# Attention and a mixture of experts on one core: where the moments, one copy and two output products stand in the queues

## The chip, the cores and the metric

The kernel runs on one core of one Trainium2 chip. A core has five engines, each with its own queue that is worked off in order: TensorE (PE, matrix products; PEld is its weight load), VectorE (DVE), ScalarE (ACT), GpSimd (POOL) and SyncE (SP), which here only issues transfers. ScalarE and GpSimd issue transfers too. The metric is the device time of one execution in microseconds (us); lower is better. All numbers are float32.

## The reference

The input has 8 sequences of 1024 rows, 256 wide. All rows are normalised, and the output is the input plus two branches of the normalised rows: a causal linear attention with 16 heads, and a mixture of 8 experts of which each row uses 2.

```python
xn = _layernorm(x, axis=-1)

# attention: q, k, v are products of xn with 256 x 256 weights, 16 heads of 16
q = jax.nn.elu(q) + 1.0
k = jax.nn.elu(k) + 1.0
kv_cumsum = jnp.cumsum(jnp.einsum('blhd,blhe->blhde', k, v), axis=1)
out = jnp.einsum('blhd,blhde->blhe', q, kv_cumsum)
denom = jnp.clip(jnp.einsum('blhd,blhd->blh', q, jnp.cumsum(k, axis=1)), 1e-06, None)
attention = (out / denom[..., None]).reshape(Bx, Lx, HIDDEN) @ Wo.T

# experts: the two best of 8 by xn @ Wr, weighted by the softmax of the two
gate = jnp.einsum('bsh,ehi->besi', xn, W1)          # W1, W3: 8 x 256 x 512
up = jnp.einsum('bsh,ehi->besi', xn, W3)
y = jnp.einsum('besi,eih->besh', jax.nn.silu(gate) * up, W2)   # W2: 8 x 512 x 256
experts = jnp.einsum('bse,besh->bsh', c, y)

return x + attention + experts
```

## The kernel before

**Blocks and tiles.** The 8192 rows are 16 blocks of 512 rows (`NBLK`), each of 4 pieces of 128 rows (`NCH`). The experts' work is in tiles of 128 rows that share one expert: `NM` = 132 tiles, of which the first `N1` = 25 are listed from the first four blocks alone (`first_batch`) and the others from all rows (`second_batch`, made while tiles 12 to 21 run).

**Of each block.** `moments(t, n)` computes mean and reciprocal deviation of n blocks on VectorE: per piece a statistics instruction (L283) and its aggregate (L284), then once per call some 17 small dependent instructions for the reciprocal square root. It reads `xb`, the loaded rows. `normalise` (L318, ScalarE for these blocks) applies them, `turn` (L333) transposes the block on TensorE and stores it, and `load_x(t + 5)` on ScalarE's queue loads a later block into the buffer that came free. `logits` (L356), `add_logits` and, every fourth block, `route` choose the experts. In the loop over tiles, tile j first normalises and turns block t = 4 + j (up to block 15).

**Attention of a block** is a generator, `block_steps`, with 9 steps. Steps 0 to 3 project q, k, v (L795, L811), turn k (L858), and make the denominators (L880 on TensorE, L886 and L887 on VectorE), which go through DRAM in five transfers on SP. Step 4 computes the first piece's `scores` (L917): products into four PSUM buffers, all that the pool `ps_mm` has, which VectorE then masks one by one into `s_sb` (L924). Steps 5 to 8 take the pieces c = 0 to 3 in turn: the scores of piece c + 1, then `weigh` of piece c (L943, L951, L961 on TensorE; `oT` L968, and the new state, L971 and L980, on VectorE). `attend` is the output product of one piece: four matmuls with `wo_sb` (L993), a copy by ScalarE into the tile `at` (L998, one buffer), and, after piece 3, one transfer by GpSimd that adds the block into DRAM (L1003): into `acc_d` for the first four blocks as long as `acc_d` has not been copied to the output, else into the output. The `attend` of piece 3 is left in the list `behind` and done in the next block's step 0, after its two q projections. `attend_upto` says how many steps are made by tile j; from tile 22 on it is some 1.14 a tile.

**Of each tile** (`ffn_step`): gathers of its rows by GpSimd four tiles ahead (L1178, L1183), its weights W1 and W3 two tiles ahead on SP (L1244, five buffers), the hidden products `gu_ps` (L1263, two PSUM buffers of `ps_mm`), SiLU on ScalarE (L1271) and the product on VectorE (L1274, `hT`), the output product `y_ps` of the tile before (L1282), its scaling on VectorE (L1289) and an adding scatter by GpSimd (L1293). From tile 27 on the rows are turned by a transfer on SP (`ffn_turn_halves`, L1209; issued with the weights of the same tile, two tiles ahead) instead of on TensorE (L1228), with a copy by VectorE ahead of it (L1200) and one by ScalarE behind it (L1218, `xgT`).

**One copy.** The first 25 tiles and the attention of the first blocks are added up in `acc_d`. At tile `N1 + 1` = 26, `acc_d` is copied to the first 2048 rows of the output by a transfer on SP (L1382), 2 MB read and 2 MB written. It has to wait for all that was added into `acc_d` before it, and what is added to the output comes after it.

**What sets the order.** Outside the first part, which is in written order, a planner puts the instructions of each engine in order at compile time: it runs the program by its own estimate of times and lets each engine take, of what is ready by that estimate, what stands first in the text. On the chip each queue then keeps that order, and an instruction that waits holds all behind it. `in_order` pins an instruction behind what stands before it on its engine; all of SP's transfers are pinned so. `tc.issue_after(ins)` puts what its block writes on `ins`'s engine behind `ins` in the queue, without waiting for its end. Before, the moments in the loop are put behind `last_token`, the last instruction of the first batch's list.

Of the kernel before, what the change touches and what calls it, by code (L numbers as in the profile page):

```python
# [51 lines left out]
ALU = mybir.AluOpType  # L52
# [12 lines left out]
def tile_attention_moe(  # L65
# [14 lines left out]
    nc = tc.nc  # L80
    B, L, H = x.shape
    E, _, I = w1.shape
# [751 lines left out]
    def project(t):  # L834


        if t > 0:
            begin(t)
            for o in range(KC):
                for _ in project_q(t, o):  # L840
                    pass
                mask_q(t, o)
                yield
            for c in range(0, NCH, 2):
                for _ in project_k(t, c):
                    pass
                yield
        else:
            for _ in range(4):
                yield  # L850
        qT, qm, kT, kn, va, rden = blocks[t]
        upto_t = two.tile([P, KC], F32, tag="upto_t", name="upto_t")
        fresh = t % BLK_PER_SEQ == 0
        qks = []
        for o in range(KC):
            tp = ps_t.tile([P, TB], F32, tag="t", name="tp")
            for c in range(NCH):
                nc.tensor.transpose(  # L858
                    tp[:, bass.ts(c, P)], kn[:, c, bass.ts(o, P)], ident
                )  # L860
            nc.scalar.copy(kT[:, o, :], tp)
            ksum = two.tile([P, TB], F32, tag="ksum", name="ksum")
            nc.vector.tensor_tensor_scan(
                ksum, ones[:, 0:1].to_broadcast([P, TB]), kT[:, o, :],
                0.0 if fresh else sums[0][:, o : o + 1], ALU.mult, ALU.add,
            )
            nc.vector.tensor_copy(upto_t[:, o : o + 1], ksum[:, TB - 1 : TB])
            nc.vector.tensor_tensor(ksum, qT[:, o, :], ksum, ALU.mult)
            qks.append(ksum)
            yield  # L870
        for c in range(0, NCH, 2):
            if t > 0:
                for _ in project_v(t, c):
                    pass
            yield

        den = ps_y.tile([P, P], F32, tag="y", name="den")
        for o in range(KC):
            for c in range(NCH):
                nc.tensor.matmul(  # L880
                    den[32 * c : 32 * c + 32, :], lhsT=own_of[:, o, :],
                    rhs=qks[o][:, bass.ts(c, P)], start=(o == 0), stop=(o == KC - 1),
                    skip_group_check=True,
                )
        over = one.tile([P, P], F32, tag="over", name="over")
        nc.vector.tensor_scalar(over, den, EPS_DEN, None, ALU.max)  # L886
        nc.vector.reciprocal(over, over)  # L887

        through = den_d[t % 2]
        for c in range(NCH):  # L890
            in_order(
                nc.sync.dma_start(
                    out=through[HEADS * c : HEADS * (c + 1)],
                    in_=over[32 * c : 32 * c + HEADS, :].unsqueeze(1).to_broadcast([HEADS, HD, P]),
                )
            )
        in_order(
            nc.sync.dma_start(
                out=rden.rearrange("p c o l -> p (c o) l"),
                in_=through.rearrange("(x h) d l -> (h d) x l", h=HALF),  # L900
            )
        )
        yield
        del xnTs[t]
        sums[0] = upto_t

    state = [None]

    def scores(t, c):

        qT, qm, kT, kn, va, rden = blocks[t]
        span = bass.ts(c, P)
        s_ps = [ps_mm.tile([P, KC, 2, P], F32, tag="mm", name="s_ps") for r in range(4)]
        for hh in range(KC):
            for r in range(4):
                rows = slice(32 * r, 32 * r + 32)
                nc.tensor.matmul(  # L917
                    s_ps[r][:, hh].rearrange("p a l -> p (a l)"), lhsT=kT[rows, hh, span],
                    rhs=qm[rows, hh, :, span], start=True, stop=True,
                )  # L920
        s_sb = []
        for r in range(4):
            sm = masked.tile([P, KC * 2, P], F32, tag="s_sb", name="s_sb")
            nc.vector.tensor_tensor(  # L924
                sm, s_ps[r].rearrange("p k a l -> p (k a) l"), causal_b, ALU.mult
            )
            s_sb.append(sm)
        return t, c, s_sb

    def weigh(t, c, s_sb):  # L930

        qT, qm, kT, kn, va, rden = blocks[t]
        first = t % BLK_PER_SEQ == 0 and c == 0
        last = t % BLK_PER_SEQ == BLK_PER_SEQ - 1 and c == NCH - 1
        span = bass.ts(c, P)
        both_ps = ps_t.tile([P, KC * P + KC * PAIR], F32, tag="t", name="o_ps")
        o_ps = both_ps[:, 0 : KC * P].rearrange("p (k l) -> p k l", k=KC)
        kv_ps = both_ps[:, KC * P :].rearrange("p (k d) -> p k d", k=KC)
        before_c = state[0]
        if not first:  # L940
            for hh in range(KC):
                for r in range(4):
                    nc.tensor.matmul(  # L943
                        o_ps[32 * r : 32 * r + 32, hh, :],
                        lhsT=before_c[:, hh, 32 * r : 32 * r + 32], rhs=qT[:, hh, span],
                        start=(hh == 0), stop=False, skip_group_check=True,
                    )
        for hh in range(KC):
            for a in range(2):
                for r in range(4):  # L950
                    nc.tensor.matmul(  # L951
                        o_ps[32 * r : 32 * r + 32, hh, :],
                        lhsT=va[:, c, 4 * hh + r, a, :],
                        rhs=s_sb[r][:, 2 * hh + a, :],
                        start=(first and a == 0), stop=(a == 1), skip_group_check=True,
                    )

        if not last:
            for hh in range(KC):
                for r in range(4):  # L960
                    nc.tensor.matmul(  # L961
                        kv_ps[32 * r : 32 * r + 32, hh, :],
                        lhsT=kn[:, c, hh * P + 32 * r : hh * P + 32 * r + 32],
                        rhs=own_v(va, c, 4 * hh + r, 4 * hh + r + 1),
                        start=True, stop=True, skip_group_check=True,
                    )
        oT = two.tile([P, KC, P], F32, tag="oT", name="oT")
        nc.vector.tensor_tensor(oT, rden[:, c], o_ps, ALU.mult)  # L968
        if not last:
            new = three.tile([P, KC, P], F32, tag="kv", name="kv")  # L970
            nc.vector.tensor_tensor(  # L971
                new.rearrange("p k (g d) -> p k g d", d=PAIR),
                kv_ps.unsqueeze(2).to_broadcast([P, KC, 4, PAIR]),
                heads.rearrange("p (g d) -> p g d", d=PAIR).unsqueeze(1).to_broadcast(
                    [P, KC, 4, PAIR]
                ),
                ALU.mult,
            )
            if not first:
                nc.vector.tensor_tensor(new, new, before_c, ALU.add)  # L980
            state[0] = new
        return oT
# [26 lines left out]
    def block_steps(t):  # L1009


        for i, _ in enumerate(project(t)):
            if i == 1 and behind:
                attend(*behind.pop())
            if i in (1, 3, 5, 8):
                yield
        if t + 1 < NBLK:
            fetch(t + 1)
        waiting = scores(t, 0)
        yield  # L1020
        done = None
        for c in range(NCH):
            coming = scores(t, c + 1) if c + 1 < NCH else None
            if done and c + 1 < NCH:
                attend(*done)
            oT = weigh(*waiting)
            if done and c + 1 == NCH:
# [308 lines left out]
    for j in range(NM + 1):  # L1336
# [7 lines left out]
            for _ in routing:  # L1344
                pass
        if 0 < j and t < NBLK:
            if j % 2 == 0:
                with tc.issue_after(last_token[0].ins):
                    for _ in moments(t, 2):
                        pass  # L1350
            normalise(t)
            turn(t)
            if t + 5 < NBLK:
# [20 lines left out]
        if j < LISTS:  # L1374
            attend_upto(3 + j // 2)
        elif j < READ:
            attend_upto(AHEAD - 3 * (READ - j - 1) // 2)
        else:
            attend_upto(AHEAD + (NBLK * STEPS - AHEAD) * (j - READ + 1) // (NM - READ - 4))
        if j == N1 + 1:  # L1380
            copied.append(j)
            in_order(nc.sync.dma_start(out=out_rows[0 : FT * P, :], in_=acc_d[:, :]))  # L1382
        ffn_step(j, LATE if N1 < j <= N1 + LATE else 0)
    assert steps_made[0] == NBLK * STEPS
    while stored[0] < NM:
        ffn_store(stored[0])
# [51 lines left out]
```

## Time and profile before

| what | value |
|---|---|
| time, median of 7 runs | 1284.06 us (1278.55 to 1287.39) |
| the profiled execution's own time | 1285.06 us |
| its span, first to last instruction | 1283.3 us |
| mean granted TensorE clock | 0.989 |
| TensorE busy, weight load busy | 1219.4 us, 1049.6 us |
| VectorE, ScalarE, GpSimd busy | 674.3, 553.8, 523.4 us |
| HBM read and written | 196.30 MB, 52.67 MB |

A line such as "L1263" is line 1263 of the kernel. A timeline's row gives the start (us from the span's start), the duration, the engine, line and operation, what is written from what, how many instructions were merged, and in brackets how long the engine was idle before and what ended the wait ("issue": nothing that the profile shows). In the lists of waits the columns are the total in us, how often, and the longest. The chain of waits is followed back from the last instruction, at each step to what released it; its rows give start, duration and what. Matmuls overlap at their ends, so distances are read from start to start. The granted clock is the share of TensorE's full clock that was given; 0.5 is half speed.

### The profile page before, as it was taken

How to read it: one execution, taken by the hardware profiler on the slowest of the kernel's cores; microseconds unless marked ns; L12 is line 12 of the kernel's file. 1: busy time of each engine (PE TensorE's matmuls, PEld its weight loads, DVE VectorE, ACT ScalarE, POOL GpSimd, SP SyncE). 2: the span in 40 equal slices, each digit the busy share in tenths (PEclk: the TensorE clock that was granted, in tenths of full speed). 3: DMA queues.
4: the chain of work that ended last, by engine and by line, in shares of the span. 5: the costliest groups of instructions: out<-in, count | busy, mean ns of one | idle time of the engine just before them, and what ended most of it. 6: DMA issues, size and time to landing. Idle time of an engine off the chain costs nothing.

```text
span 1283.3 us, 30887 instructions
## 1 busy us (share of the span) xinstructions
PE 1219.4 (95%) x12102; PEld 1049.6 (82%) x12102; DVE 674.3 (53%) x1541; ACT 553.8 (43%) x1060; POOL 523.4 (41%) x460
## 2 busy tenths in 40 slices
PE   5689999999999999999999999999999999999995
PEld 4568887778888888888888888888888888888885
DVE  7766579863344454535453544445454536354541
ACT  5565465371532526262625344252626262444420
POOL 3633334323444444344343435444434435343432
PEclk9899999999999999999999999999999999999998
DMA  9797565557798798889696979988788979787984
GB/s 339 256 290 226 174 191 154 188 135 241 181 234 199 179 210 188 208 187 220 161 222 158 225 164 216 191 173 229 175 208 193 213 166 216 171 219 161 204 194 68
DMA packets 220593, 254.30 MB, mean 198 GB/s; under 512 B 73218, under 2 KB 144514, under 8 KB 220162
## 3 DMA queue, kind: packets, MB, share of 16 engines
q1 hardware_dynamic: 177058, 198.08, 53.2%
q0 software_dynamic: 38064, 43.22, 24.1%
q10 hardware_dynamic: 5328, 11.01, 2.4%
q8 instruction: 99, 1.62, 0.5%
q14 instruction: 44, 0.36, 0.1%
HBM read 196.30 MB, written 52.67 MB: 194 GB/s over the span
## 4 chain that ended last, share of the span: by engine, by line
PE 86%; DVE 6%; DMA 4%; ACT 2%; SPq 1%; issue 1%; POOL 0%; POOLq 0%; ACTq 0%; DVEq 0%
PE gu_ps L1263 37%; PE y_ps L1282 17%; PE a_ps L993 5%; PE s_ps L917 5%; PE o_ps L951 4%; PE zkv L811 4%; PE zkk L811 4%; PE zq L795 4%; PE o_ps L943 2%; DMA xb<-in_x_dram 1%; DMA acc_d<-in_x_dram 1%; PE tp L858 1%; DVE s_sb L924 1%; DVE at_place L573 1%; SPq L1138 1%
## 5 line engine op out<-in xcount | busy, mean ns | idle before, releaser
L1263 PE MATMUL gu_ps<-xgT,w 128*128 128x128 f32 x4224 | 513.7, 279 | 18.9 <-DVE s_sb L924 12.0
L1263 PEld LDWEIGHTS gu_ps<-xgT,w 128*128 128x128 f32 x4224 | 494.1, 194 | 35.6 <-DVE s_sb L924 16.4
L1293 POOL DMA_INDIRECT out_dram<-y,dst_i x107 | 177.2, 1656 | 282.1 <-issue 56.8
L1282 PE MATMUL y_ps<-w_sb,hT 128*128 x1056 | 250.8, 380 | 1.4 <-DVE hT L1274 1.4
L1178 POOL DMA_INDIRECT xg<-in_x_dram,src_i x132 | 128.7, 975 | 288.9 <-DVE half L1200 160.1
L1271 ACT ACTIVATE hT<-gu_ps 128x512 f32<-128x512 f32 x132 | 78.8, 597 | 318.7 <-PE gu_ps L1263 318.3
L1282 PEld LDWEIGHTS y_ps<-w_sb,hT 128*128 128x128 f32 x1056 | 190.3, 190 | 23.2 <-DVE hT L1274 1.0
L924 DVE TENSOR_TENSOR s_sb<-s_ps,causal 128x512 f32<-128x512 f32 x256 | 162.6, 682 | 71.6 <-PE o_ps L951 40.0
L1274 DVE TENSOR_TENSOR hT<-gu_ps,hT 128x512 f32<-128x512 f32 x132 | 90.4, 685 | 69.6 <-PE gu_ps L1263 44.1
L1183 POOL DMA_INDIRECT entry<-tab_d,of_i x107 | 106.4, 994 | 38.7 <-issue 32.2
L1289 DVE TENSOR_SCALAR y<-y_ps,entry 128x256 f32<-128x256 f32 x132 | 63.6, 482 | 111.3 <-PE y_ps L1282 111.0
L1200 DVE COPY half<-xg 128x512 uint16<-128x512 uint16 x105 | 45.7, 435 | 139.9 <-ACT xg L1190 139.8
L998 ACT COPY at<-a_ps 128x256 f32<-128x256 f32 x64 | 23.6, 369 | 156.6 <-PE a_ps L993 156.6
L917 PE MATMUL s_ps<-qm,kT 32*128 32x256 f32 x1024 | 85.8, 403 | 0.5 <-DVE hT L1274 0.4
L1218 ACT COPY xgT<-halfT 128x512 uint16<-128x512 uint16 x105 | 79.6, 758 | 3.2 <-DMA halfT<-half 3.2
L1190 ACT ACTIVATE xg<-xg,entry 128x256 f32<-128x256 f32 x132 | 78.6, 596 | 4.7 <-DMA xg<-in_x_dram,src_i 4.7
L993 PE MATMUL a_ps<-wo_sb,oT 128*128 128x256 f32 x256 | 70.0, 396 | 2.1 <-DVE oT L968 2.1
L917 PEld LDWEIGHTS s_ps<-qm,kT 32*128 32x128 f32 x1024 | 51.2, 184 | 24.5 <-issue 19.6
L951 PE MATMUL o_ps<-s_sb,va 128*32 128x128 f32 x2048 | 68.9, 273 | 0.0
L1293 POOL DMA_INDIRECT acc_d<-y,src_i x25 | 42.8, 1712 | 59.2 <-DVE y L1289 25.7
L993 PEld LDWEIGHTS a_ps<-wo_sb,oT 128*128 128x128 f32 x256 | 44.7, 189 | 24.1 <-issue 14.5
L811 PE MATMUL zkk<-wkv_sb,xnT 128*128 128x256 f32 x256 | 59.5, 381 | 0.0
(213 smaller groups left out, 1331.3 us busy)
## 6 DMA issues: line engine op xcount, KB each, us to landing
w<-in_w_dram SPq DMA_DIRECT2D x264, 512.0 KB
den_d<-over SPq DMA_DIRECT2D x64, 128.0 KB
rden<-den_d SPq DMA_DIRECT2D x16, 512.0 KB
xnT_d<-xnT ACTq DMA_DIRECT2D x15, 512.0 KB
xnT<-xnT_d SPq DMA_DIRECT2D x15, 512.0 KB
out_dram<-in_x_dram SPq DMA_DIRECT2D x12, 512.0 KB
out_dram<-at POOLq DMA_DIRECT2D x12, 512.0 KB, 9.6
xb<-in_x_dram SPq DMA_DIRECT2D x10, 512.0 KB
```

The lines of the kernel that those rows point to most:

```text
L811: nc.tensor.matmul(z[:, i, :], lhsT=xnTs[t][:, k, bass.ts(c + i, P)], rhs=wkv_sb[:, k, a, :], start=(k == 0), stop=(k == KC - 1),)
L917: nc.tensor.matmul(s_ps[r][:, hh].rearrange("p a l -> p (a l)"), lhsT=kT[rows, hh, span], rhs=qm[rows, hh, :, span], start=True, stop=True,)
L924: nc.vector.tensor_tensor(sm, s_ps[r].rearrange("p k a l -> p (k a) l"), causal_b, ALU.mult)
L951: nc.tensor.matmul(o_ps[32 * r : 32 * r + 32, hh, :], lhsT=va[:, c, 4 * hh + r, a, :], rhs=s_sb[r][:, 2 * hh + a, :], start=(first and a = ...
L993: nc.tensor.matmul(a_ps, lhsT=oT[:, hh, :], rhs=wo_sb[:, hh, :], start=(hh == 0), stop=(hh == 1),)
L1178: nc.gpsimd.indirect_dma_start(out=xg[j], out_offset=None, in_=x_rows[:, :], in_offset=bass.IndirectOffsetOnAxis(ap=src_i[:, i : i + 1], a ...
L1183: nc.gpsimd.indirect_dma_start(out=entry[j], out_offset=None, in_=table[:, :], in_offset=bass.IndirectOffsetOnAxis(ap=num_i[:, i : i + 1], ...
L1218: nc.scalar.copy(xgT[j].bitcast(U16).rearrange("p k (l b) -> p b k l", b=2), halves.pop(j).rearrange("p (b k) l -> p b k l", b=2),)
L1263: done = nc.tensor.matmul(ps[:, i, :], lhsT=w13[:, k, bass.ts(i, P)], rhs=xgT[j][:, k, :], start=(k == 0), stop=(k == KC - 1),)
L1274: nc.vector.tensor_tensor(hT, gu[1], hT, ALU.mult)
L1282: done = nc.tensor.matmul(y_ps, lhsT=hT[:, i, :], rhs=w2_sb[:, bass.ds(e * (IC * H) + i * H, H)], start=(i == 0), stop=(i == IC - 1),)
L1293: nc.gpsimd.indirect_dma_start(out=rows[:, :], out_offset=bass.IndirectOffsetOnAxis(ap=dst_i[:, i : i + 1], axis=0), in_=ys.pop(j), in_off ...
```

## The change

Four things are moved; the arithmetic stays.

- The moments in the loop: instead of a call for blocks t and t + 1 ahead of `normalise(t)` in tiles 2, 4, 6, 8 and 10, there are calls after the attention steps of tiles 0 (block 6), 2, 4, 6, 8 (blocks 7 and 8, 9 and 10, 11 and 12, 13 and 14) and 10 (block 15). They are put behind `last_masked`, the attention's VectorE instruction written last (`over`, `s_sb` or `oT`); in tile 0 behind `last_token` as before.
- The copy from `acc_d` to the output is written behind `ffn_step(26)`, whose transfers on SP are tile 28's weights and its transpose.
- The output product of a block's piece 3 is written behind the next block's first scores (step 4) instead of in its step 0.
- The output product of piece 1 is written ahead of the scores of piece 3 instead of behind them.

```diff
         nc.vector.tensor_scalar(over, den, EPS_DEN, None, ALU.max)
-        nc.vector.reciprocal(over, over)
+        last_masked[0] = nc.vector.reciprocal(over, over)
...
     state = [None]
+    last_masked = [None]
...
             sm = masked.tile([P, KC * 2, P], F32, tag="s_sb", name="s_sb")
-            nc.vector.tensor_tensor(
+            last_masked[0] = nc.vector.tensor_tensor(
...
-        nc.vector.tensor_tensor(oT, rden[:, c], o_ps, ALU.mult)
+        last_masked[0] = nc.vector.tensor_tensor(oT, rden[:, c], o_ps, ALU.mult)
...
         for i, _ in enumerate(project(t)):
-            if i == 1 and behind:
-                attend(*behind.pop())
             if i in (1, 3, 5, 8):
                 yield
         if t + 1 < NBLK:
             fetch(t + 1)
         waiting = scores(t, 0)
+        if behind:
+            attend(*behind.pop())
         yield
         done = None
         for c in range(NCH):
+            if c == 2:
+                attend(*done)
             coming = scores(t, c + 1) if c + 1 < NCH else None
-            if done and c + 1 < NCH:
+            if c == 1:
                 attend(*done)
             oT = weigh(*waiting)
...
         if 0 < j and t < NBLK:
-            if j % 2 == 0:
-                with tc.issue_after(last_token[0].ins):
-                    for _ in moments(t, 2):
-                        pass
             normalise(t)
             turn(t)
...
+        if j % 2 == 0 and j + 1 < LISTS:
+            ahead = (t + 2, 1) if j == 0 else (t + 1, min(2, NBLK - t - 1))
+            with tc.issue_after((last_masked if j else last_token)[0].ins):
+                for _ in moments(*ahead):
+                    pass
+        ffn_step(j, LATE if N1 < j <= N1 + LATE else 0)
         if j == N1 + 1:
             copied.append(j)
             in_order(nc.sync.dma_start(out=out_rows[0 : FT * P, :], in_=acc_d[:, :]))
-        ffn_step(j, LATE if N1 < j <= N1 + LATE else 0)
```

## The prediction

> **What bounds the kernel now.** I read the page first, then TensorE's waits, then the chain of waits and the timelines around each wait.
>
> ```profile
> PE 1219.4 (95%) x12102; PEld 1049.6 (82%) x12102; DVE 674.3 (53%) x1541; ACT 553.8 (43%) x1060; POOL 523.4 (41%) x460
> ...
> PE 86%; DVE 6%; DMA 4%; ACT 2%; SPq 1%; issue 1%; POOL 0%; POOLq 0%; ACTq 0%; DVEq 0%
> ```
>
> TensorE works 95% of the span and carries 86% of the chain. The change removes no matmul, so all it can win is TensorE's idle time (64 us, some 25 of them in the first 60 us and 12 behind the last matmul, which nothing here touches), time at a reduced clock, and small losses where one kind of matmul follows another. The waits of TensorE, 320 to 1230 us (waited for: us in total, times, longest):
>
> ```profile
> PE gu_ps L1263 <- DVE s_sb L924: 5.3, 8, 0.7
> PE gu_ps L1263 <- issue: 4.0, 5, 0.8
> PE gu_ps L1263 <- ACT xgT L1218: 2.0, 1, 2.0
> ```
>
> The first two are one place, once in each of blocks 3 to 15: 13 waits, 9.3 us. After a block's first scores there is nothing behind them on TensorE but the next tile's `gu_ps`, whose PSUM buffer is held until VectorE has masked `s_ps`. On TensorE's timeline (start, us, engine, line):
>
> ```profile
> 652.23 1.15 PE L917 MATMUL s_ps<-qm,kT 32*128 32x256 f32 x16
> 654.18 3.81 PE L1263 MATMUL gu_ps<-xgT,w 128*128 128x128 f32 x32 [0.81 <-issue]
> ...
> 692.05 1.03 PE L993 MATMUL a_ps<-wo_sb,oT 128*128 128x256 f32 x4
> 692.92 1.28 PE L1263 MATMUL gu_ps<-xgT,w 128*128 128x128 f32 x10
> ```
>
> The last two rows are the output product of the block's last piece, at a place where TensorE waits for nothing: it takes 692.92 - 692.05 = 0.87 us there.
>
> The third wait comes from SP's queue. Its waits and its timeline:
>
> ```profile
> SPq L1382 <- DMA acc_d<-at: 9.8, 1, 9.8
> ```
>
> ```profile
> 337.63 0.39 SPq L1244 DMA_DIRECT2D w<-in_w_dram  x1
> 347.96 0.55 SPq L1382 DMA_DIRECT2D out_dram<-acc_d  x1
> 349.12 1.07 SPq L1244 DMA_DIRECT2D w<-in_w_dram  x1
> 350.24 1.32 SPq L1209 DMA_TRANSPOSE halfT<-half  x1
> ```
>
> The rows' copy stands 9.8 us at the head of SP's queue until block 2's attention has been added into `acc_d`. Tile 28's weights and transpose are behind it. The chain then runs 8.70 us through that transpose, ends in the 2.0 us wait, and tile 28's 32 `gu_ps` matmuls take 5.46 us instead of 3.8.
>
> The longest wait behind the start is at 88.46 us, 5.90 us, after the first scores of block 0. VectorE's timeline and the chain there:
>
> ```profile
> 86.11 0.29 DVE L406 TENSOR_TENSOR same<-lg_all,best 128x128 f32<-128x128 f32 x1
> 90.27 0.43 DVE L283 BATCH_NORM_STATS2 st<-xb 128x6 f32<-128x256 f32 x1 [3.87 <-DMA xb<-in_x_dram]
> ...
> 93.63 0.68 DVE L924 TENSOR_TENSOR s_sb<-s_ps,causal 128x512 f32<-128x512 f32 x1
> ```
>
> ```profile
> 94.36 5.06 PE gu_ps L1263 x22
> ...
> 107.37 2.65 PE gu_ps L1263 x22
> ```
>
> The moments of block 12 wait in VectorE's queue for a load of x that was issued at 80.80. The masks are behind them, so `gu_ps` starts at 94.36. Then 22 matmuls take 5.06 us where 22 take 2.65 later: the granted clock is 0.65 from 94.4 to 103.0, which is 0.35 x 8.6 = 3.0 us lost. Likewise it is 0.73 from 360 to 366, 0.27 x 6 = 1.6 us, after the 2.0 us wait.
>
> **1. Moments behind attention's VectorE work.** Block 12's moments move from the planner's early place to behind piece 0's `oT` (tile 6; at 118 before), long after their load. Without them the queue from 86.40 holds eight routing and eviction steps that cost 1.8 us interleaved (chain pieces 0.28 + 0.40 + 0.19 + 0.19 + 0.19 + 0.18 + 0.24 + 0.13) and some 2.5 us alone, as dependent steps add 0.03 to 0.1 us each. The first mask then runs from 88.9 to 89.5 and `gu_ps` starts at 89.6: 94.36 - 89.6 = 4.8 us. The wait left is 1.1 us, and waits up to 1.37 us (at 240.3) show no lower clock, so the 3.0 us go too: 7.8 us. The ceiling is 5.9 + 3.4 (the clock loss from 93.6 on) = 9.3.
>
> What it costs: moments now come one tile ahead of their use. A pair of blocks takes VectorE 8 x 0.48 (statistics and their aggregate) + 17 x 0.20 (the square root's chain) = 7.2 us; `normalise` adds 4 x 0.5 on ScalarE. Queued behind them on VectorE are the tile's `hT` and `y`; waiting for them are `normalise`, the transposes of `turn`, and through `turn` the ACT-issued load of x five blocks on, which still has some 10 us. Six calls instead of five add 17 x 0.20 = 3.4 us, covered by VectorE's idle time from 130 to 160 us. Of these, one end shows: before, `turn(15)` ran at 163.99, 3.25 us behind piece 2's last VectorE step (160.74); now 4 x 0.48 + 3.4 + 2.0 = 7.3 us lie between, so routing and the second batch's lists start 4.1 us later against TensorE. From 180 to 260 VectorE is 91% busy and TensorE waits for it in small pieces. Bounds: 0 (TensorE has other work) to 4.1 us; I take 2.0, the middle, as both are nearly full there. Net gain 5.8 us.
>
> **2. The copy behind a tile's weights.** `w(28,0)` and its transpose can then go at 339.4, when tile 25's last weights come free, and `w(28,1)` at 344.4. The output product of block 2's last piece also moves from tile 26 to tile 29, after the copy; so it is added to `out_dram` and the copy waits only for tile 24's store (issued 336.22, landing median 6.3 us). `xgT(28)` is then limited by ScalarE, whose SiLU of tile 27 ends at 355.8; with 0.76 us it is there at 356.6, before the preceding transposes end at 357.75. Gain 2.0 + 1.6 = 3.6 us; bound 0 if the transpose is still late. The copy's 4 MB move some 3 us earlier, the scatter into `out_dram` with them.
>
> The Trainium skill, "TensorE: Matmul & The Clock Gate", Part 1, has the clock fall only after an idle window of about 3.4 us. The row above disagrees: 2.0 us sufficed. By the page this term would be 2.0 instead of 3.6 and the forecast 1.6 us higher.
>
> **3. The last piece's output product behind the next block's first scores.** At step 0 the 0.87 us go. At step 4 `s_ps` to `gu_ps` takes 654.18 - 652.23 = 1.95 us now. With the product between: 1.08 (677.00 to 678.08 below) + 0.97 (`a_ps` to `gu_ps` behind narrow matmuls, 406.44 to 407.41) = 2.05, while the mask is ready at 1.95. Net 0.87 - 0.10 = 0.77 us, 13 times: 10.0 us. Blocks 1 and 2 have no such gap (`y_ps` lies there): 0. Bounds 0 to 13 x 0.87 = 11.3.
>
> Each moved product brings its ScalarE copy and POOL's add along. `at` has one buffer. Now its copy ends near 725.3, POOL's store and gather put the add's issue near 726.8, it lands 9.6 us later (row of part 6), at 736.4; the next block's first copy into `at` comes at 740.1. Even if the add waited for the store issued at 723.85 to land (5.7 us), it would land at 739.2. ScalarE's next work behind that copy is a SiLU at 743.7. So 0 us; it costs once it is 4 us later still. POOL's store behind the add waits for it as now (7.7 us), with rows gathered four tiles ahead.
>
> **4. Piece 1's product ahead of piece 3's scores.** Now:
>
> ```profile
> 677.00 1.15 PE L917 MATMUL s_ps<-qm,kT 32*128 32x256 f32 x16
> 678.08 1.13 PE L993 MATMUL a_ps<-wo_sb,oT 128*128 128x256 f32 x4
> 679.14 0.64 PE L943 MATMUL o_ps<-qT,kv 128*32 128x128 f32 x16
> ```
>
> `a_ps` costs 1.06 us between two narrow kinds (679.14 - 678.08); behind `y_ps` it is wide after wide, 0.87. 0.2 us, 13 times: 2.6 us; bounds 0 to 2.6.
>
> **Sum.** 5.8 + 3.6 + 10.0 + 2.6 = 22.0 us. The profiled execution took 1285.06 us (span 1283.3), 1.0 above the median of 1284.06. 1284.06 - 22.0 = 1262.
>
> **Rivals.** (a) Slower: the wait moves from the masks to the transposes. If the planner keeps `turn` ahead of the next tile's `gu_ps`, TensorE meets it 5.9 us after the tile before starts (3.84 + 0.38 + 1.73), but piece work ends 1.3 us in, and moments and `normalise` need 9.2 more: 4.6 us each for four pairs and 2.7 for the single block 15, 21 us, with 1.6 us of clock each 29. Less 7.8 + 3.6 + 12.6 that is 5 us slower, 1289; it decides from 4 us a call. For it: all ten blocks' moments now sit one tile from use. Against it: the planner already splits `tp` and puts `lg_ps` inside `gu_ps` by readiness. (b) The product lands ahead of the scores, as the planner takes what is ready; then its 0.87 us only moves and 13 gaps stay: 1272. Against: in pieces 1 and 2 the order written is scores, product, and so it ran. (c) The early gain is given back wholly by the late lists and transposes: 1268. (d) The copy's order alone does nothing, the transpose limits it: 1266.
>
> **How the numbers follow.** Likeliest case 0.62: 1262, own range 1256 (ceilings 9.3 + 3.6 + 11.3 + 2.6 = 26.8, less a little spread) to 1270 (4.1 us of lists, no gain from 4, part of 2 missing). (b) 0.10; (c), (d) and mixtures of them 0.10; several failing at once, within 0.3% of no change, 0.05; (a) and its like 0.13. Range 1256 to 1278, which takes in (b), (c) and (d) mixed. Faster 0.82, same 0.05, slower 0.13; 0.3%, 3.9 us, is about what a measurement of this kernel can tell.
>
> **What would show it.** Right: no `st` waits for x ahead of an `s_sb`; clock full at 94 to 103 and 360 to 366; no L1382 wait ahead of `w(28)`; `s_ps`, `a_ps`, `gu_ps` without a gap once a block, and blocks 69.3 instead of 70.3 us apart. Wrong: TensorE waits at `tp` L333 for `xb` L318, `a_ps` ahead of the first `s_ps`, ScalarE's `at` waiting for the add, or wider gaps from 180 to 300 us.

## The result, and the profile after

The changed kernel takes 1297.57 us (median of 19 runs, 1288.85 to 1305.37) against 1283.46 us (46 runs of the kernel before beside it, 1278.55 to 1289.18): a ratio of 1.0102, 95% interval 1.0087 to 1.0117. By the ratio that is 13 us slower, where 22 us faster was forecast. The profiled execution took 1296.67 us, with a span of 1295.0 us and a mean clock of 0.979 (1285.06, 1283.3 and 0.989 before). Line numbers shift: `gu_ps` is L1266, `y_ps` L1285, `a_ps` L994, `s_ps` L918, `s_sb` L925, `oT` L969, the copy L1387.

Engines and the chain of waits, from the page after:

```profile
PE 1226.5 (95%) x12102; PEld 1053.0 (81%) x12102; DVE 680.1 (53%) x1558; ACT 557.3 (43%) x1062; POOL 522.3 (40%) x460
...
PE 80%; DMA 9%; DVE 7%; ACT 2%; issue 1%; SPq 1%; POOL 0%; POOLq 0%; DVEq 0%; ACTq 0%
```

TensorE still works 95% of the span, but the chain has moved: TensorE carries 80% instead of 86%, transfers 9% instead of 4%. So a transfer that was hidden is no longer hidden. TensorE's waits from 320 to 1230 us (total, times, longest) name it:

```profile
PE a_ps L994 <- DVE oT L969: 6.8, 6, 2.0
PE gu_ps L1266 <- DVE s_sb L925: 0.4, 1, 0.4
```

Of the 13 waits of 9.3 us behind the scores one of 0.4 us is left, about as forecast, and the wait for `xgT` is gone. In their place stand six waits for `oT`. Both on TensorE's timeline:

```profile
534.36 1.15 PE L918 MATMUL s_ps<-qm,kT 32*128 32x256 f32 x16
537.54 1.39 PE L994 MATMUL a_ps<-wo_sb,oT 128*128 128x256 f32 x4 [2.04 <-DVE oT L969]
...
661.91 1.15 PE L918 MATMUL s_ps<-qm,kT 32*128 32x256 f32 x16
662.99 1.13 PE L994 MATMUL a_ps<-wo_sb,oT 128*128 128x256 f32 x4
663.96 3.73 PE L1266 MATMUL gu_ps<-xgT,w 128*128 128x128 f32 x32
```

The last three rows are what the change wanted, in block 7: scores, product and next tile without a gap, 2.05 us from `s_ps` to `gu_ps`, just the 1.08 + 0.97 of the prediction. The first two are the new loss, in block 5. The timelines of VectorE, GpSimd and SP there:

```profile
519.02 0.95 DVE L887 RECIPROCAL over<-over 128x128 f32<-128x128 f32 x1
...
537.07 0.42 DVE L969 TENSOR_TENSOR oT<-rden,o_ps 128x256 f32<-128x256 f32 x1 [3.35 <-DMA rden<-den_d]
```

```profile
522.46 1.41 POOL L1004 DMA_DIRECT2D out_dram<-at  x1 [1.41 <-DMA out_dram<-y,dst_i]
```

```profile
527.60 0.37 SPq L898 DMA_DIRECT2D rden<-den_d  x1
```

`oT` needs the denominators back from DRAM. They come 18.0 us after their reciprocal here, where it took 13.2 to 14.9 us in blocks 3 to 14 of the kernel before and 15.3 in block 15. In between, at 522.46 us, GpSimd issues the 512 KB add of the previous block, which the moved product brought along. In this block the four writes end in the usual time (the read is issued 8.6 us behind the reciprocal, 7.3 to 8.9 before) and the read is late, 9.4 us from issue to landing instead of 5.7 to 7.3. In blocks 3, 6 and 14 it is the writes that are late: the read is issued 10.5 to 11.4 us behind the reciprocal.

At the start, the masks are no longer held, but TensorE waits elsewhere (first TensorE's longest wait from 60 to 130 us, then VectorE's timeline, last the row of before for block 7):

```profile
PE tp L333 <- ACT xb L318: 4.6, 2, 4.3
```

```profile
77.11 0.69 DVE L283 BATCH_NORM_STATS2 st<-xb 128x6 f32<-128x256 f32 x2
...
83.70 0.68 DVE L925 TENSOR_TENSOR s_sb<-s_ps,causal 128x512 f32<-128x512 f32 x1
...
86.73 0.15 DVE L305 SCALAR_TENSOR_TENSOR tab<-mv,tab 128x8 f32<-128x8 f32 x1
```

```profile
48.34 0.39 DVE L283 BATCH_NORM_STATS2 st<-xb 128x6 f32<-128x256 f32 x1
```

The moments of blocks 7 and 8 begin at 77.11 us, behind the denominators' reciprocal; before, block 7's ran from 48.34. They end at 86.9, ScalarE normalises only then, and TensorE waits 4.3 us for the transposes of block 7. The clock is at half for 13.7 us (84.3 to 98.0) instead of 6.8 (93.6 to 100.4), and tile 4 starts at 98.1 us instead of 94.36.

The second batch's lists begin later as well. Their first VectorE step, before and after:

```profile
175.42 0.16 DVE L517 TENSOR_SCALAR rows_i<-count 128x8 int32<-128x8 f32 x1
```

```profile
186.75 0.16 DVE L517 TENSOR_SCALAR rows_i<-count 128x8 int32<-128x8 f32 x1
```

The copy, on SP's timeline, no longer waits at the head of the queue:

```profile
355.63 0.39 SPq L1247 DMA_DIRECT2D w<-in_w_dram  x1
356.13 0.55 SPq L1387 DMA_DIRECT2D out_dram<-acc_d  x1
```

The start of tiles, after less before, shows where it all lies: +3.7 us at tile 4, some +12 from tile 16 to 23, +7.3 at tile 29 (the copy's gain, and the clock is full from 360 to 366), then slow gains eaten by the `oT` waits, +4.3 at the last tile. The last matmul ends at 1275.34 instead of 1271.04, but the end comes 19.6 us behind it instead of 12.2; this stretch is called the tail below. On GpSimd's timeline:

```profile
1222.37 1.40 POOL L1004 DMA_DIRECT2D out_dram<-at  x1 [4.54 <-DMA out_dram<-y,dst_i]
...
1282.99 1.54 POOL L1296 DMA_INDIRECT out_dram<-y,dst_i  x1 [2.95 <-DMA out_dram<-y,dst_i]
1287.54 1.55 POOL L1296 DMA_INDIRECT out_dram<-y,dst_i  x1 [3.00 <-DMA out_dram<-y,dst_i]
```

Every write to the output waits for the one ahead of it to land, some 4.5 us a store. Block 14's add is issued at 1222.37 (1180.92 before), in the stretch where tiles start 5.3 us apart, so that the chain of writes makes up little of a delay.

So the theory after the traces: moments too late, about +12; copy about -3.7; products -11, with +8.5 given back by late denominators and +7.4 by the tail. The rivals: the parts hinder one another at the start; or the `oT` waits come from the changed order on VectorE and TensorE, not from the add.

### The profile page after: what moved, and what is told of

It is laid out like the page before. It is cut to its first block, busy times and chain, and to the rows that moved or that the text cites. A ratio compares the mean times of both kernels' runs of the same rounds, so it can differ in the third digit from the quotient of the medians.

```text
span 1295.0 us, 30936 instructions
## 1 busy us (share of the span) xinstructions
PE 1226.5 (95%) x12102; PEld 1053.0 (81%) x12102; DVE 680.1 (53%) x1558; ACT 557.3 (43%) x1062; POOL 522.3 (40%) x460
## 4 chain that ended last, share of the span: by engine, by line
PE 80%; DMA 9%; DVE 7%; ACT 2%; issue 1%; SPq 1%; POOL 0%; POOLq 0%; DVEq 0%; ACTq 0%
PE gu_ps L1266 33%; PE y_ps L1285 15%; PE a_ps L994 4%; PE zq L795 4%; PE zkv L811 4%; PE o_ps L952 4%; PE zkk L811 4%; DMA rden<-den_d 4%; DMA den_d<-over 4%; PE s_ps L918 4%; PE o_ps L944 2%; PE tp L333 1%; PE tp L858 1%; DMA out_dram<-y,dst_i 1%; DVE s_sb L925 1%
## 5 line engine op out<-in xcount | busy, mean ns | idle before, releaser
L1266 PE MATMUL gu_ps<-xgT,w 128*128 128x128 f32 x4224 | 508.1, 278 | 1.3 <-DVE s_sb L925 0.8
L1266 PEld LDWEIGHTS gu_ps<-xgT,w 128*128 128x128 f32 x4224 | 491.9, 193 | 17.4 <-issue 9.9
L1285 PE MATMUL y_ps<-w_sb,hT 128*128 x1056 | 253.3, 383 | 3.2 <-PE lg_t L377 1.9
L1285 PEld LDWEIGHTS y_ps<-w_sb,hT 128*128 128x128 f32 x1056 | 191.4, 191 | 26.4 <-PE lg_t L377 2.5
L925 DVE TENSOR_TENSOR s_sb<-s_ps,causal 128x512 f32<-128x512 f32 x256 | 162.8, 682 | 70.2 <-PE s_ps L918 45.4
L918 PE MATMUL s_ps<-qm,kT 32*128 32x256 f32 x1024 | 89.9, 404 | 1.1 <-DVE hT L1277 0.9
L994 PE MATMUL a_ps<-wo_sb,oT 128*128 128x256 f32 x256 | 70.7, 399 | 10.0 <-DVE oT L969 9.9
L918 PEld LDWEIGHTS s_ps<-qm,kT 32*128 32x128 f32 x1024 | 52.8, 184 | 27.0 <-issue 20.5
L1296 POOL DMA_INDIRECT acc_d<-y,src_i x25 | 42.4, 1698 | 65.9 <-DVE s_sb L925 15.4
L994 PEld LDWEIGHTS a_ps<-wo_sb,oT 128*128 128x128 f32 x256 | 45.1, 191 | 25.5 <-DVE oT L969 11.8
L952 PEld LDWEIGHTS o_ps<-s_sb,va 128*32 128x32 f32 x2048 | 57.7, 111 | 3.6 <-issue 3.0
```

The costliest lines, as they stand in the source:

```text
L918: nc.tensor.matmul(s_ps[r][:, hh].rearrange("p a l -> p (a l)"), lhsT=kT[rows, hh, span], rhs=qm[rows, hh, :, span], start=True, stop=True,)
L925: last_masked[0] = nc.vector.tensor_tensor(sm, s_ps[r].rearrange("p k a l -> p (k a) l"), causal_b, ALU.mult)
L952: nc.tensor.matmul(o_ps[32 * r : 32 * r + 32, hh, :], lhsT=va[:, c, 4 * hh + r, a, :], rhs=s_sb[r][:, 2 * hh + a, :], start=(first and a = ...
L994: nc.tensor.matmul(a_ps, lhsT=oT[:, hh, :], rhs=wo_sb[:, hh, :], start=(hh == 0), stop=(hh == 1),)
L1266: done = nc.tensor.matmul(ps[:, i, :], lhsT=w13[:, k, bass.ts(i, P)], rhs=xgT[j][:, k, :], start=(k == 0), stop=(k == KC - 1),)
L1285: done = nc.tensor.matmul(y_ps, lhsT=hT[:, i, :], rhs=w2_sb[:, bass.ds(e * (IC * H) + i * H, H)], start=(i == 0), stop=(i == IC - 1),)
```

## The experiments

Ratios are against the kernel before, run on the same chip beside each, with 95% intervals.

**Moments alone**, the change's own edit (calls behind the attention steps, tied to `last_masked`):

> Only the moments part of the change; the copy and the output products stay as in the kernel before. Theory A (what the two traces say): the change's loss at the start is the moments'. Their moving puts PE's wait ahead of tile 4 on the normalise, leaves 13.7 us at half clock instead of 6.8 (+3.7 us at tile 4), and the lists come 11.5 us later, all of which the tiles from the 15th on pass to the end: +11 to +12.5 us, about 1295, first weight load of tile 16 some 12 us later than before and the same distance at the last matmul. Theory B (the prediction's first term): 7.8 gained, 2.0 given back by late lists, about 1278. Theory C: the start is delayed by the three parts together (gap products lengthen block 1's and 2's steps), and the moments alone cost 3 to 5 us: 1287 to 1289.

Measured 1296.32 us, ratio 1.0094 (1.0065 to 1.0122): +12. Theory A. The wait for the normalise is there again (4.4 us); its tile starts run +3.4 us at tile 4, +10.3 at tile 15, +9.9 at tile 20, +10.6 at the last tile. Nearly all of the loss is there once the lists run, and nothing later returns any of it. This profile, of an execution of 1304.95 us, also has a tail of 21.6 us, though its products and block 14's add stand where they stood before.

**Moments a step earlier**, tied to what attention's VectorE work has written by then:

```diff
-        if j % 2 == 0 and j + 1 < LISTS:
-            ahead = (t + 2, 1) if j == 0 else (t + 1, min(2, NBLK - t - 1))
+        if (j == 0 or j % 2) and j + 2 < LISTS:
+            ahead = (t + 2, 1 if j == 0 else min(2, NBLK - t - 2))
```

> Only the moments part, with every pair taken one step earlier still (so that the normalise of the next step finds its numbers ready), behind the masks as in the change. Theory A1 (the loss is the wait of the normalise for moments that come too late): PE's wait of 4.4 us for the turn of block 7 goes, its half clock with it, tile 4 starts at 90 instead of 97.7, and the time is 1278 to 1284. Theory A2 (the loss is the order of VectorE: the masks and moments before route and logits, so that the lists come late whatever the pair's step): lists again 8 to 11 us late, 1290 to 1296.

Measured 1280.25 us, ratio 0.9981 (0.9963 to 0.9998). A1. But "behind the masks as in the change" holds only for the later pairs: by tile 1 attention has written neither reciprocal nor mask, so the pair of blocks 7 and 8 stands behind `last_token`, and its statistics start at 50.02 us, as before. TensorE's waits from 60 to 130 us are now only these:

```profile
PE gu_ps L1264 <- DVE s_sb L925: 1.5, 1, 1.5
PE cnt_ps L443 <- DVE both L429: 0.2, 1, 0.2
```

Tile 4 starts at 90.4 (4 us earlier than before), and the second batch's first VectorE step at 172.7 (175.4 before, 186.8 with the change). After the wait of 1.5 us the clock is still at half from 91.6 to 98.5 us.

**Moments untied**: the change's place in the program, but tied only to `last_token`:

```diff
-            with tc.issue_after((last_masked if j else last_token)[0].ins):
+            with tc.issue_after(last_token[0].ins):
```

> The moments part of the change alone, at the change's place in the program, but tied only to the second batch's last token as before, not to the masks and oT of attention. Theory A3 (the tie makes the moments late, and with them the normalise and the lists): the statistics of blocks 7 and 8 start at about 50 us as before instead of 77, PE's wait for the normalise goes, 1280 to 1286. Theory A4 (the place in the program's order does it): they start at 70 us or later and the time is 1291 to 1298.

Measured 1310.5 us where the kernel before, beside it, took 1309.46: ratio 1.0012 (0.9988 to 1.0036). A3: at this place in the program it is the tie that makes the moments late. VectorE's first row for block 7, untied here and tied in the kernel with the moments alone:

```profile
49.72 0.42 DVE L283 BATCH_NORM_STATS2 st<-xb 128x6 f32<-128x256 f32 x1
```

```profile
77.04 0.69 DVE L283 BATCH_NORM_STATS2 st<-xb 128x6 f32<-128x256 f32 x2
```

Untied, the planner takes the moments two to three tiles ahead of their use, as before, and the mask's wait returns too (6.9 us). TensorE also waits 4.9 us for a normalise, but for that of block 5, up to 64.85 us; the kernel of the same series that leaves the moments as before (below, the 128 KB added at once) has 3.6 us there too. The changed kernel's wait ahead of block 7's transposes is gone, as expected.

**One block's moments a step**, at before's place:

```diff
-            if j % 2 == 0:
+            if j > 1:
                 with tc.issue_after(last_token[0].ins):
-                    for _ in moments(t, 2):
+                    for _ in moments(t, 1):
```

> Before's place of the moments, but one block's moments a step instead of a pair every second step; all else as before. The trace of before has VectorE idle for 3.9 us ahead of the statistics of the pair's second block at 90.3 us, which is what holds the masks back. Theory A (it waits there for the rows of the next block, not for VectorE's work): the 5.9 us wait of PE shrinks below 2 us and its half-clock stretch goes, -5 to -8 at tile 4; five more calls of 3 us each on VectorE give back 0 to 4: 1276 to 1284. Rival (the wait is VectorE's work ahead of the masks): the wait stays at 4 us or more, 1284 to 1292.

Measured 1290.92 us, ratio 1.0055 (1.0034 to 1.0075). The rival's numbers, but by neither reason. On VectorE:

```profile
94.42 0.43 DVE L283 BATCH_NORM_STATS2 st<-xb 128x6 f32<-128x256 f32 x1 [4.22 <-DMA xb<-in_x_dram]
```

It waits for block 12's own rows, the first of the pair, so asking for fewer blocks does not help. In this kernel, with its extra calls, ScalarE issues the load at 84.9 instead of 80.8, and TensorE waits 5.2 us for the masks.

**The copy alone**, behind `ffn_step(26)`:

> Only the copy of the first rows goes behind the tile's weight load on SP; all else as before. Theory A and the prediction's second term agree: PE's wait of about 2.1 us at 359 and its half-clock stretch go, -3.6 us (bounds -2.1 and -3.7), about 1280. Rival (the prediction's case that the copy does nothing, its wait being replaced by the next one): 0, 1283.5.

Measured 1283.15 us, ratio 0.9981 (0.9961 to 1.0000): -2.4, the interval holding -3.6. In its profile the step from tile 27 to tile 29 is 3.9 us shorter than before, and the clock is full from 360 to 366 us.

**Piece 3's product alone**, behind the next block's first scores:

> Only piece 3's output product goes from the next block's projections to behind the next block's first scores. Theory A (the traces): 0.77 to 0.95 us gained in each of 13 blocks, 10 to 12 in all; given back by PE's waits for oT in the blocks in which the rows' add is issued 2.6 to 3.5 us behind the denominators (rden lands 1.5 to 4 us later), 6 to 8.5 in all, and by a GpSimd queue that runs late at the end, up to 7.4: between -4 and +6, middle +3, about 1286; the tail behind the last matmul 17 to 20 us against 12.2. Theory B (the prediction's third term, neither wait nor tail): -10, about 1274.

Measured 1284.99 us, ratio 1.0022 (0.9997 to 1.0047): +2.8. Theory A: the last tile starts 6.9 us earlier than before, and the tail behind the last matmul takes 19.7 us.

**The same, last block put back:**

```diff
         for i, _ in enumerate(project(t)):
+            if i == 1 and behind and t + 1 == NBLK:
+                attend(*behind.pop())
```

> The product of piece 3 behind the next block's scores alone, but the last block keeps the place of before (block 14's last product and its add of 512 KB run among block 15's projections). Theory A: the tail of the gap kernel is block 14's add, which comes some 30 us later (1211.6 against 1180.9) into the stretch in which every write to the output waits for the one ahead of it; put back, the tail behind the last matmul falls from 19.6 to about 12 us: -7 us against the gap kernel, -5 against before, about 1279. Rival: the tail is late because all stores run late through the steady state; then it stays and the time is 1285.

Measured 1282.9 us, ratio 0.9993 (0.9970 to 1.0016). The tail takes 11.8 us in this profile, as Theory A has it. That block 14's add makes the tail is still not shown. In the profiles with the add moved (the change, this kernel without the mend, the change without its moments) the tail is 19.6, 19.7 and 16.7 us. In 11 of the 13 other profiles of this document it is 11.8 to 15.4, but the two left have 21.6 (the moments alone) and 20.5 (the whole change mended, below), with the add early:

```profile
1172.88 1.40 POOL L1004 DMA_DIRECT2D out_dram<-at  x1 [2.32 <-ACT at L999]
```

The total moved by 3.7 us, and the two intervals overlap. In this profile the `oT` waits came to 9.8 us against 4.9; how often the add and the denominators meet varies.

**The add a step later**, on top of that kernel, with one buffer as before:

```diff
+        if c == NCH - 1 and t < NBLK - 2:
+            adds.append((t, at))          # issued by add_rows()
...
             oT = weigh(*waiting)
+            if c == 0 and adds:
+                add_rows()
```

> As the kernel with the last block put back, and the rows' add of every other block is issued behind the next block's first weighing, a step later, when the denominators' rows have landed. Theory A (the add's 512 KB beside the denominators' small packets make oT late): PE's waits for oT, 6.5 us with one stretch at half clock in the gap kernel, fall below 2 us; the denominators land 13 to 15 us behind their reciprocal in every block; -11 us against before, about 1273. Rival B (oT is late since VectorE's or TensorE's order changed, not by the add): the waits stay at 6 us or more and the time stays at about 1279. Rival C (the single buffer of the rows: ScalarE's copy then waits for the add's landing): new waits of 1 us or more per block on ScalarE and what it feeds, 1280 to 1290.

Measured 1317.58 us, ratio 1.0280 (1.0251 to 1.0310): rival C, and worse than its number. The denominators now land 13.3 to 15.0 us behind the reciprocal in blocks 4 to 15 with no `oT` late there, which speaks for A. But the add holds the single `at` (ScalarE's waits, TensorE's waits):

```profile
ACT at L998 <- DMA out_dram<-at: 105.3, 10, 11.7
```

```profile
PE s_ps L917 <- DVE hT L1287: 16.5, 11, 1.6
```

ScalarE stands 10 us at a time in front of a copy, SiLU stands behind it, then `hT`, then TensorE.

**Rows of piece 3 in a tile of their own.** The memory taken is the same; the buffer is cut in two:

```diff
-        if c == 0:
-            ats[t] = one.tile([P, NCH, H], F32, tag="at", name=f"at{t}")
+        if c == 0:
+            ats[t] = one.tile([P, NCH - 1, H], F32, tag="at", name=f"at{t}")
+        elif c == NCH - 1:
+            ats[t] = one.tile([P, 1, H], F32, tag="at3", name=f"at3_{t}")
...
+        elif c == NCH - 2:                # pieces 0 to 2, 384 KB
+            nc.gpsimd.dma_start(out=to[t][:, 0 : c + 1, :], in_=at, accum_op=ALU.add)
+        elif c == NCH - 1:                # piece 3, 128 KB: add_rows()
+            adds.append((t, at))
```

> Piece 3's product behind the next block's scores, the last block as before; the rows of pieces 0 to 2 and of piece 3 have tiles of their own, in the same memory. The add of pieces 0 to 2 (384 KB) is issued behind piece 2's product, that of piece 3 (128 KB) behind the next block's first weighing. Theory A (the add's collision with the denominators makes oT late, and nothing else takes the gain): PE's waits for oT from 380 us on fall below 2 us in all, ScalarE's waits for the add as in before, the gain of 0.8 us a block stays: -8 to -11 against before, 1273 to 1276. Rival B (a part of the gain lies in work that VectorE or GpSimd must do anyway): -1 to -4, about 1281. Rival C (more adds in the chain of writes to the output make the stores and the gathers behind them late): 1284 or more.

Measured 1271.33 us, ratio 0.9913 (0.9892 to 0.9934): -11. Theory A. Block 11 in this kernel, TensorE's timeline:

```profile
931.16 1.15 PE L917 MATMUL s_ps<-qm,kT 32*128 32x256 f32 x16
932.24 1.13 PE L995 MATMUL a_ps<-wo_sb,oT 128*128 128x256 f32 x4
```

and the same place where only the product was moved:

```profile
937.20 1.15 PE L917 MATMUL s_ps<-qm,kT 32*128 32x256 f32 x16
938.73 1.13 PE L993 MATMUL a_ps<-wo_sb,oT 128*128 128x256 f32 x4 [0.39 <-DVE oT L968]
```

From 360 us on no wait for `oT` is left in the list. Tile 24 starts 2.1 us earlier than before and the last one 14.8; 3.3 of that gain is at tiles 28 and 29, so 9.3 us are the 12 blocks from there on, 0.78 each.

**The same, the 128 KB added at once:**

```diff
             adds.append((t, at))
-            if t == NBLK - 2:
-                add_rows()
+            add_rows()
...
-            if c == 0 and adds:
-                add_rows()
```

> As the kernel with piece 3's rows in their own tile, but its add (128 KB) is issued as soon as the rows are there, some 3 us behind the denominators' reciprocal, where the change issues 512 KB. Theory A1 (the size of the add is what delays the denominators): the delay from the reciprocal to the issue of the denominators' read, 7.2 us without and 9 to 11 us with 512 KB beside it, stays below 8 us; PE's waits for oT from 380 us on 0 to 2 us; 1271 to 1274, as with the late add. Theory A2 (an add beside them delays them whatever its size): 9 to 11 us again, waits of 5 us or more, 1277 to 1282.

Measured 1296.47 us against 1309.46 beside it, ratio 0.9907 (0.9873 to 0.9940): as with the late add. From the reciprocal to the issue of the denominators' read it takes 7.1 to 8.9 us in all of blocks 3 to 15 (7.3 to 8.9 in the kernel before), where the 512 KB in the kernel with piece 3's product alone make it up to 11.3, and no `oT` wait is in the list. The seven blocks with the add beside the writes lie in the upper part of that range, 8.2 to 8.9, but the denominators land 13.3 to 15.1 us behind the reciprocal there and 14.3 to 15.4 in the other six. So the late issue isn't needed: the size decides (the 8 us expected as a bound was too tight, since the kernel before passes it as well).

**Piece 1's product alone:**

> Only piece 1's output product goes ahead of piece 3's scores; all else as before. Prediction's fourth term: 0.2 us in each of 13 blocks, -2.6, about 1281. Rival: the product waits there for its oT or the scores behind it are late for the masks, 0 to +3, 1284 to 1287.

Measured 1281.29 us, ratio 0.9982 (0.9962 to 1.0001): -2.3. In its profile the distance to before shrinks by 0.2 us a block, from +1.2 us at tile 29 to -1.2 at the last.

**The change without its moments:**

> The whole change but for the moments, which stay where they were. Theory A: start as before (tile 16 within 1 us of before), copy -3.6, steady state -11 + 8.5, tail +7.4: between -2 and +3, about 1284.5. Theory C (the parts together delay the start): 1288 to 1290. The prediction's terms without its first: 3.6 + 10.0 + 2.6 gained, about 1268.

Measured 1280.9 us, ratio 0.9969 (0.9944 to 0.9995): -4. The profiled execution took 1290.68 us.

**The whole change, mended**: moments a step earlier and the last block put back; then with piece 3's tile as well:

> The whole change with two mends: the moments' pairs one step earlier, and the last block's products where they were before. Theory A: start as in the kernel with early moments (-2.5), copy -2 to -3.5, piece 1's product -2.6, piece 3's product with its collisions -0.5 to -3: -8 to -12 against before, 1272 to 1276, and 22 to 25 under the change. Rival (the parts hinder each other at the start, as 17 us of moments beside the other three against 11 alone could mean): 1279 to 1285.

> The same, with the rows of piece 3 in their own tile and added behind the next block's first weighing. Theory A: -2.5 for the start, -2 to -3.5 for the copy, -2.6 for piece 1, -8 to -11 for piece 3: -15 to -19 against before, 1265 to 1269, PE's waits for oT below 3 us from 380 us on. Rival (the split costs as much as the collision): as the kernel without the split, 1272 to 1276.

Measured 1277.18 us, ratio 0.9949 (0.9927 to 0.9970), and 1266.0 us, ratio 0.9864 (0.9840 to 0.9889): 17 us faster than before and 30 faster than the change. The chain of waits of the last:

```profile
PE 88%; DVE 6%; DMA 2%; SPq 1%; ACT 1%; issue 1%; POOL 0%; POOLq 0%; ACTq 0%; DVEq 0%
```

## Why the prediction was wrong

**1. Moments: the failing step, forecast 5.8 gained, measured 12 lost.** The wait and what held it were read rightly: the masks no longer stand behind a load. The gain can be had too: in the two mended kernels, whose clock stays full there, tile 5 starts 7.9 and 7.6 us earlier than before, near the 7.8 forecast, though other parts of the change are in them as well. With the moments alone a step earlier it is 3.5; there the clock fell after a wait of 1.5 us, where the prediction had it stay full.

What failed is the cost, "moments now come one tile ahead of their use ... Of these, one end shows". The prediction priced block 15's moments alone and put the delays of all earlier pairs at nothing. Blocks 7 to 9 had their moments at 48 to 53 us, two to three tiles ahead of use, a slack that the trace of before shows and the tie took away. The lists begin 11.3 us late (the two L517 rows) and end 11.5 late (their last step, L606, starts at 298.0 instead of 286.5). Of the 11.3 us, 4.3 lie between piece 2's last VectorE step and block 15's logits, where 4.1 was forecast and the middle, 2.0, taken. Another 5.8 were there already: that VectorE step ends at 166.55 instead of 160.73. The last 1.2 come in the routing.

From 180 to 230 us VectorE is busy 48.3 of 50 us in the trace of before, which fits that all of the delay is passed on; "the middle, as both are nearly full" had no ground. Rival (a) named the right mechanism and place, `tp` for `xb`, but priced it at 4.6 us for each of four pairs; it came once at that size (4.3 us, with 6.9 us more at half clock). That the wait ahead of tile 4 and the late lists are the moments' doing is shown by the kernels with the moments alone, a step earlier and untied; how the 5.8 us added up, pair by pair, is not.

**2. Copy: right, 3.6 against 3.7 in the changed kernel's trace and 3.9 with the copy alone**, though the interval of its time reaches to zero. The Trainium skill's "TensorE: Matmul & The Clock Gate", Part 1, would have made it 2.0; the trace decides for the row. Another case came with the change: after the 2.04 us wait at 535.5 the clock is 0.57 from 538 to 542. The copy's part and piece 3's overlap: piece 3's product alone also clears this wait (its tiles 28 and 29 gain 3.7 us), because block 2's add leaves `acc_d`.

**3. Piece 3's product: right in its gain, wrong in what was costed at nothing.** 0.77 us a block was forecast, and the kernel with a tile of its own measured 0.78. The step that failed is "So 0 us". First, "each moved product brings its ScalarE copy and POOL's add along" was held against the `at` buffer and GpSimd's queue, at one place in steady state; that the add now starts 2.7 to 3.4 us behind the denominators' reciprocal in 7 of 13 blocks, beside their five transfers, was not looked at. `oT` had 0.8 to 2.5 us of slack, and in these blocks the denominators land 1.9 to 3.3 us later than before. The waits for `oT` came to 4.9 to 10.4 us in the profiles of the kernels that keep the 512 KB add at this place; with 128 KB there, or with the add a step later in two tiles, they are gone. The Trainium skill's "DMA: Bandwidth & Descriptors", Queues, rings and completion order, has each DMA engine alternate between the queues that have work, packet by packet. The rows here fit such sharing (beside the add the way to the denominators' read grows from at most 8.9 to as much as 11.4 us, or the read from at most 7.3 to 9.4), though no run looks at single packets. Second, block 14's add was not followed to the end, where the changed kernel's tail is 7.4 us longer; as the tail is also long in two profiles with the add early, its cause stays open. "It costs once it is 4 us later still" held for ScalarE's copy into `at`: moved a step later, it cost 36 us.

**4. Piece 1's product: right**, 2.3 against 2.6, though the interval reaches to zero.

**The sum.** Of the 35 us between the forecast and the measurement the moments make 18 and piece 3's product 13. The parts alone give 12.1 - 2.4 + 2.8 - 2.3 = +10.2; the clearing at tile 28 is in both the copy's and piece 3's number and counts once, which puts back 3.3 to 3.7: about +13.7, against +13.1 measured. Adding the moments to the other three parts costs 17 (1.0102 against 0.9969), alone 12; and those three parts measured -4 together where their own numbers make +1.6. With intervals of 3 to 4 us on each, these differences are not settled.

## What to carry to other kernels

An order that ties an instruction behind another is paid by its consumer: before moving one, list for every instance, not only the one that stalls, how long its result lies ready before use. Moving a product moves its transfer too: look which other transfers start within some 15 us of its new place, who needs them and with how much slack. Before a longer tail is put down to one transfer, look at the tails of other profiles: here they run from 11.8 to 21.6 us. When a collision is found, shrinking the transfer (128 KB instead of 512) was worth more than delaying it behind a single buffer.

## What the hardware showed unexpectedly

The clock also fell to half from 220.8 to 227.7 us in the changed kernel, with no TensorE wait above 0.7 us between 210 and 232 us; from 217 to 221 us TensorE was busy 2.87 of 4 us, idle in small pieces. That alone doesn't explain it: from 394.9 to 398.3 us TensorE was busy 1.61 of 3.4 us, and the clock stayed full.

An accumulating transfer of 512 KB beside the denominators' four 128 KB writes and 512 KB read made the denominators land 15.6 to 18.0 us behind their reciprocal in the changed kernel, where its other blocks from 4 on have 13.6 to 14.7. With 128 KB no difference in the landing can be told. How much TensorE waits at such meetings varies: the kernel with the last block put back lost 9.8 us in its profiled run, the one without 4.9, with the instructions in the same order in those blocks.
